# Issuing the work of two Mamba stages in a set order on each engine

## The chip, the cores and the metric

One NeuronCore of a Trainium2 chip runs the whole program. The metric is the device time of one execution in microseconds. The kernel before takes 16,464.6 us (median of four runs, 16,463.5 to 16,470.9). Executions of one kernel mostly agree here within 0.2%, and every run told below was of the fast state.

## The reference, cut to what matters

The program has three parts. Two of them are built on the Mamba recurrence: first two Mambas over one normalised input (4 images of 4096 steps), then one Mamba inside a block with two layer norms, a depthwise convolution and an MLP (4 images of 64 x 64). The third, a stage of windows, isn't touched.

```
def _mamba(x, ...):
    xc, z = split(x @ in_w.T)
    xc = silu(conv(xc) + conv_b)
    dt, B, C = split(xc @ x_w.T);  dt = softplus(dt @ dt_w.T + dt_b)
    # for every step t, 384 channels d, 16 states n:
    h = exp(dt[t] * A) * h + (dt[t] * xc[t]) * B[t]
    y[t] = sum over n of h * C[t]
    return ((y + D * xc) * silu(z)) @ out_w.T
```

Every step is float32. The recurrence can't be reordered along t; 384 x 16 rows of it are independent.

## The kernel before

A *unit* is 512 steps of one Mamba: 64 units in stage one (32 pairs, two Mambas for each piece of input), 32 in stage two. In a unit there are 12 *quads* of four scans. A quad goes through all the engines: a product on VectorE, four decays on ScalarE (Exp, into one of three buffers in PSUM, where this kernel also puts the results of its matmuls), four scans on VectorE, a multiplication with C on GpSimd (the *read* of h), and a sum over n on TensorE. One scan with its decay is a *tile*, 48 in a unit.

```
def scan(self, u, first, background):                 # one unit, cut
    for c in range(ND):
        for i, (o, q) in enumerate(...):              # a quad
            ... load dtE, dtxE ...
            nc.vector.tensor_tensor(h, dtxE, B, ALU.mult)              # product
            for j in range(4):
                nc.scalar.activation(dA, dtE[:, j, :], AF.Exp, scale=A)  # decay
                nc.vector.tensor_tensor_scan(h[:, j, :], dA, h[:, j, :], state, ...)
                background.step()                     # one piece of other work
            nc.vector.tensor_copy(self.state[:, n, :], h[:, :, T - 1])
            nc.gpsimd.tensor_tensor(h, h, C, ALU.mult)                 # read
            ... four matmuls: the sum ...
        nc.vector.scalar_tensor_tensor(y, xc, D, ys, ...)              # skip
    background.drain()
    nc.gpsimd.tensor_tensor(y, y, z, ALU.mult)                         # gate
```

All other work (norms, projections, convolution, Silu, Softplus, MLP) is a generator whose pieces are issued one after each scan. The *front* of a unit is what must be done before its scans, the *back* and *tail* are what comes after.

Of the kernel before, what the change touches and what calls it, by code (L numbers as in the profile page):

```python
# [119 lines left out]

class Norm:
# [98 lines left out]
class Mamba:  # L220
# [3 lines left out]
    def __init__(self, nc, name, taps, ins, const, work, psum, psum_y, psum_a, dram, ident, ex):  # L224
# [24 lines left out]

    def front(self, xn, first, u):  # L250

        nc, K = self.nc, self.taps
# [5 lines left out]
        for e in range(2 * ND):  # L258
            ps = self.psum.tile([128, T], F32, name="ps_in", tag="mm")
            for k in range(2):  # L260
                nc.tensor.matmul(  # L261
                    ps, self.in_w[:, k, bass.ts(e, 128)], xn[:, k, :], start=(k == 0), stop=(k == 1)
                )
            nc.scalar.copy(raw[:, e, K - 1 :] if e < ND else z[:, e - ND, :], ps)  # L264
            yield
        nc.gpsimd.tensor_copy(self.halo, raw[:, :, T:])
        xc = u["xc"] = self.work.tile([128, ND, T], F32, name="xc", bufs=2)
        for d in range(ND):
# [5 lines left out]
            nc.scalar.activation(xc[:, d, :], ps, AF.Identity, bias=self.conv_b[:, d : d + 1])  # L274
            yield
# [7 lines left out]
        nc.scalar.copy(dbl, ps)  # L283
# [3 lines left out]
        for d in range(ND):  # L287
            ps = self.psum.tile([128, T], F32, name="ps_dt", tag="mm")
            nc.tensor.matmul(ps, self.dt_w[:, bass.ts(d, 128)], dbl[:RK, :], start=True, stop=True)
            nc.scalar.activation(dt[:, d, :], ps, AF.Identity, bias=self.dt_b[:, d : d + 1])  # L290
        yield
        nc.scalar.activation(dt, dt, AF.Softplus)  # L292
        u["rows"] = []
        for i, v in enumerate((dt, dtx)):
            if i:
                nc.gpsimd.tensor_tensor(dtx, dt, xc, ALU.mult)  # L296
            r = self.dram.tile([DI, T], F32, name=("r_dt", "r_dtx")[i], bufs=3)
            u["rows"].append(r)
            rows = r.rearrange("(c q dd j) t -> q j dd c t", c=ND, q=2, j=4)
            for q in range(2):  # L300
                for j in range(4):
                    p = 32 * j + 16 * q
                    nc.sync.dma_start(rows[q, j], v[p : p + 16])
            yield

    def spread(self, u):

        nc = self.nc
        u["B"], u["C"] = [], []
        for o in range(2):  # L310
            B = self.psum_a.tile([128, T], F32, name=f"B{o}", bufs=1)
            nc.tensor.matmul(B, self.ex.spread[:, o, :], u["dbl"], start=True, stop=True)
            u["B"].append(B)
            ps = self.psum.tile([128, T], F32, name="ps_C", tag="mm")
            nc.tensor.matmul(ps, self.ex.spread[:, 2 + o, :], u["dbl"], start=True, stop=True)
            Cs = self.work.tile([128, T], F32, name=f"C{o}", bufs=2)
            nc.scalar.copy(Cs, ps)
            u["C"].append(Cs)

    def scan(self, u, first, background):  # L320
        nc = self.nc
        if first:
            nc.vector.memset(self.state, 0.0)
        self.spread(u)
        y = u["y"] = self.work.tile([128, ND, T], F32, name=f"{self.name}_y", bufs=1)
        xc, z = u["xc"], u["z"]
        at = 0
        for c in range(ND):
            ys = self.psum_y.tile([128, T], F32, name="y")
            octets = (0, 1) if c % 2 == 0 else (1, 0)  # L330
            for i, (o, q) in enumerate([(o, q) for o in octets for q in range(2)]):
                if i < 2:
                    wide = []
                    for r, n in zip(u["rows"], ("dtE", "dtxE")):
                        t = self.work.tile([128, 4, T], F32, name=n, bufs=2)
                        row = c * 128 + q * 64
                        nc.sync.dma_start(
                            t,
                            r[row : row + 64, :]
                            .rearrange("(dd j) t -> dd (j t)", j=4)  # L340
                            .unsqueeze(1)
                            .broadcast_to([16, 8, 4 * T]),
                        )
                        wide.append(t)
                    u[q] = wide
                dtE, dtxE = u[q]
                n = (c * 2 + o) * 2 + q
                h = self.work.tile([128, 4, T], F32, name="h", bufs=3)
                nc.vector.tensor_tensor(  # L349
                    h, dtxE, u["B"][o].unsqueeze(1).broadcast_to([128, 4, T]), ALU.mult  # L350
                )
                for j in range(4):
                    dA = self.psum_a.tile([128, T], F32, name="dA", bufs=3)
                    nc.scalar.activation(dA, dtE[:, j, :], AF.Exp, scale=self.A[:, n, j : j + 1])  # L354
                    nc.vector.tensor_tensor_scan(  # L355
                        h[:, j, :], dA, h[:, j, :], self.state[:, n, j : j + 1], ALU.mult, ALU.add
                    )
                    background.step()
                nc.vector.tensor_copy(self.state[:, n, :], h[:, :, T - 1])  # L359
                nc.gpsimd.tensor_tensor(  # L360
                    h, h, u["C"][o].unsqueeze(1).broadcast_to([128, 4, T]), ALU.mult
                )
                for j in range(4):
                    nc.tensor.matmul(  # L364
                        ys[32 * j : 32 * j + 32, :],
                        self.ex.gather[:, q, :],
                        h[:, j, :],
                        start=(i == 0),
                        stop=(i == 3),
                    )  # L370
            nc.vector.scalar_tensor_tensor(  # L371
                y[:, c, :], xc[:, c, :], self.D[:, c : c + 1], ys, ALU.mult, ALU.add
            )
        background.drain()
        nc.gpsimd.tensor_tensor(y, y, z, ALU.mult)  # L375


def two_mambas(tc, x, g, b, m_ins, ex_aps, out):
# [3 lines left out]
    with ExitStack() as ctx:  # L382
# [9 lines left out]
        eps = const.tile([128, 1], F32, name="eps")  # L392
        nc.vector.memset(eps, EPS)
# [3 lines left out]
        ex = Expand(nc, const, *ex_aps)  # L397
        mambas = [
            Mamba(nc, f"m{i}", 4, m_ins[i], const, work, psum, psum_y, psum_a, dram, ident, ex)
# [8 lines left out]
        def norm(u):  # L408
# [7 lines left out]
            nc.scalar.activation(rs, mv[:, :, 1], AF.Sqrt, bias=eps)  # L416
            nc.vector.reciprocal(rs, rs)
            yield
            xs = u["xs"] = work.tile([128, nq, C], F32, name="xs", bufs=2)
            for q in range(nq):  # L420
                nc.vector.tensor_scalar(
# [6 lines left out]
                )  # L428
            for i, op in ((0, ALU.mult), (1, ALU.add)):
# [5 lines left out]
            for k in range(2):  # L435
# [5 lines left out]
                nc.scalar.copy(xT[:, k, :], ps)  # L441
                yield

        def front(u, i):
            if i == 0:
                yield from norm(u)
            u[i] = {}
            yield from mambas[i].front(u["xT"], u["t"] == 0, u[i])

        def back(u):  # L450
            o = work.tile([128, nq, C], F32, name="o", bufs=2)
            for q in range(nq):
# [10 lines left out]
                nc.vector.tensor_tensor(o[:, q, :], ps, u["xs"][:, q, :], ALU.add)  # L463
                yield
            rows = out[u["b"], bass.ts(u["t"], T), :]
            nc.sync.dma_start(rows.rearrange("(q p) c -> p q c", p=128), o)
            yield

        background = Background()
        units = [{"b": bi, "t": t} for bi in range(NB) for t in range(NT)]  # L470
        load(units[0])
# [488 lines left out]
```

## Time and profile before

| part | us | a unit |
|---|---|---|
| stage one, first scan 98 to last skip 7676 | 7578 | 118 |
| stage two, 7798 to last scan 12,897 | 5099 | 159 |
| windows | 3395 | - |

In the views PE is TensorE, DVE VectorE, ACT ScalarE, POOL GpSimd, and SPq the queue of the sync engine, which issues the transfers; L355 is line 355 of the kernel. The two views below are VectorE's waits, in the kernel before: in each line stands the waiting instruction, whom it waited for, the sum in us, how often, and the longest. First stage one (500 to 7500 us):

```profile
DVE h L355 <- ACT dA L354: 789.4, 72, 25.5
DVE m_y L371 <- PE y L364: 381.6, 120, 7.2
DVE h L349 <- PE y L364: 129.4, 82, 5.9
```

then stage two (8000 to 12,500 us, some 27 units):

```profile
DVE ln_d L140 <- PE mean L138: 525.5, 40, 23.1
DVE img L559 <- PE ps_out L552: 416.2, 53, 45.9
DVE m_y L371 <- PE y L364: 278.3, 48, 21.1
```

In stage one a few long waits for the decay (72, up to 25 us) make up about half of VectorE's idle 1627 us. In stage two no wait is the main one: norm, output projection and skip each take 10 to 19 us of a unit. Keep these names for the comparison: after the change the names are others and the sum is much the same.

### The profile page before, as it was taken

The page shows a single profiled execution, that of the slowest core. Times are in us where ns is not written, and L with a number is a line of the kernel's source. Part 1 is how long each engine was busy: PE and PEld are TensorE (multiplying, and loading weights), DVE is VectorE, ACT ScalarE, POOL GpSimd, SP SyncE. Part 2 cuts the span into 40 slices and gives each one's busy share as a digit, 9 for nine tenths or more (in the row PEclk, how much of TensorE's full clock was granted, in tenths as well). Part 3 has the DMA queues.
Part 4 walks back from the last instruction along what each step waited for, and adds up shares of the span by engine and source line. Part 5 has one row for each costly group of instructions (what it writes and reads, how often), then busy time and mean ns, then how long its engine had stood idle before and what let it go on. Part 6 is the DMA issues. An engine that isn't in the chain of part 4 may idle for free.

```text
span 16446.6 us, 96745 instructions
## 1 busy us (share of the span) xinstructions
PE 11089.0 (67%) x34064; PEld 4801.7 (29%) x34064; DVE 9585.2 (58%) x9115; ACT 6342.4 (39%) x8392; POOL 6089.1 (37%) x1714
## 2 busy tenths in 40 slices
PE   5555556555555555565677777677777498998989
PEld 1112112111211211121222222222222165655656
DVE  6777877877787787786665656555656411112120
ACT  4444444444444444443444445444444211111111
POOL 4555555555555555554443434433434100000000
PEclk7666666666666666666677777777777699998989
DMA  5555555555555555554444444434434200000000
GB/s 129 118 120 118 128 120 119 127 120 119 119 126 120 117 125 122 120 130 105 106 94 89 93 88 94 101 82 92 97 88 90 53 10 6 10 6 10 6 2 6
DMA packets 366749, 1449.36 MB, mean 88 GB/s; under 512 B 95402, under 2 KB 128462, under 8 KB 218710
## 3 DMA queue, kind: packets, MB, share of 16 engines
q1 hardware_dynamic: 365502, 1440.02, 39.7%
q8 instruction: 268, 4.39, 0.1%
q10 hardware_dynamic: 760, 3.16, 0.1%
q14 instruction: 219, 1.79, 0.0%
HBM read 1254.25 MB, written 188.74 MB: 88 GB/s over the span
## 4 chain that ended last, share of the span: by engine, by line
PE 38%; DVE 28%; POOL 12%; DMA 8%; issue 7%; ACT 6%; SPq 0%; POOLq 0%; ACTq 0%; DVEq 0%
DVE h L355 18%; POOL h L360 10%; PE plus L726 6%; PE minus L726 5%; DVE h L349 5%; DMA dtE<-r_dt 4%; PE y L364 4%; DMA dtxE<-r_dtx 3%; PE ps_h L187 3%; PE ps_dw L576 3%; PE ps_conv L271 3%; PE ps_in L261 3%; PE ps_o L196 3%; POOL m_y L375 2%; ACT dA L354 2%
## 5 line engine op out<-in xcount | busy, mean ns | idle before, releaser
L360 POOL TENSOR_TENSOR h<-h,C 128x2048 f32<-128x2048 f32 x1152 | 5204.0, 4517 | 4399.1 <-DVE m_state L359 4207.4
L355 DVE TENSOR_TENSOR_SCAN h<-dA,m_state,h 128x512 f32<-128x512 f32 x4608 | 5556.8, 1263 | 1121.4 <-ACT dA L354 1115.1
L354 ACT ACTIVATE dA<-dtE,m_A 128x512 f32<-128x512 f32 x4608 | 3097.3, 687 | 3839.3 <-DVE h L355 2923.3
L364 PE MATMUL y<-h,gather 128*32 128x512 f32 x9216 | 1976.0, 900 | 3440.0 <-POOL h L360 3287.0
L349 DVE TENSOR_TENSOR h<-dtxE,B 128x2048 f32<-128x2048 f32 x1152 | 2612.2, 2273 | 622.4 <-PE y L364 277.7
L364 PEld LDWEIGHTS y<-h,gather 128*32 128x32 f32 x9216 | 226.9, 128 | 4812.9 <-POOL h L360 4369.9
L726 PE MATMUL plus<-xn,t 96*96 96x256 f32 x4352 | 1013.6, 380 | 0.0
L261 PE MATMUL ps_in<-xT,m_in_w 96*128 96x512 f32 x1536 | 848.1, 694 | 214.5 <-ACT z L264 197.5
L271 PE MATMUL ps_conv<-raw,m_conv 128*128 128x512 f32 x2112 | 980.6, 616 | 7.7 <-ACT z L264 6.6
L737 DVE TENSOR_TENSOR y<-plus,neg 96x512 f32<-96x512 f32 x64 | 44.0, 687 | 1597.1 <-ACT neg L736 1597.1
L726 PE MATMUL minus<-xn,t 96*96 96x256 f32 x3840 | 922.8, 392 | 10.8 <-ACT xn L169 10.7
L187 PE MATMUL ps_h<-xn,t 96*128 96x512 f32 x1536 | 802.1, 666 | 79.9 <-ACT xn L169 69.3
L726 PEld LDWEIGHTS plus<-xn,t 96*96 96x96 f32 x4352 | 710.1, 163 | 338.4 <-issue 133.1
L196 PE MATMUL ps_o<-hid,t 128*96 128x512 f32 x1536 | 739.3, 638 | 53.4 <-ACT hid L192 53.4
L726 PEld LDWEIGHTS minus<-xn,t 96*96 96x96 f32 x3840 | 638.2, 168 | 244.0 <-ACT xn L169 26.6
L664 POOL MEMSET img<- 96x132 f32 x4 | 0.8, 206 | 1788.2 <-DVE xw L711 1788.2
L371 DVE SCALAR_TENSOR_TENSOR m_y<-xc,m_pack,y 128x512 f32<-128x512 f32 x288 | 212.7, 738 | 738.8 <-PE y L364 738.8
L456 PE MATMUL ps_out<-m_pack,m_y 128*128 128x192 f32 x1536 | 413.7, 439 | 289.1 <-POOL m_y L375 184.0
L147 PE MATMUL var<-mean_w,xn 96*128 96x1 f32 x2048 | 357.4, 304 | 371.8 <-ACT xn L142 371.8
L271 PEld LDWEIGHTS ps_conv<-raw,m_conv 128*128 128x128 f32 x2112 | 416.0, 200 | 585.7 <-issue 547.4
L140 DVE TENSOR_TENSOR ln_d<-x,mean 96x1024 f32<-96x1024 f32 x96 | 116.5, 1214 | 744.3 <-PE mean L138 744.2
L296 POOL TENSOR_TENSOR dt_dtx<-dt_dtx,xc 128x1536 f32<-128x1536 f32 x96 | 329.2, 3429 | 551.7 <-ACT dt_dtx L292 551.7
(120 smaller groups left out, 11402.0 us busy)
## 6 DMA issues: line engine op xcount, KB each, us to landing
dtE<-r_dt SPq DMA_DIRECT2D x576, 1024.0 KB, 8.9
dtxE<-r_dtx SPq DMA_DIRECT2D x576, 1024.0 KB, 7.3
r_dt<-dt_dtx SPq DMA_DIRECT2D x768, 96.0 KB, 3.3
r_dtx<-dt_dtx SPq DMA_DIRECT2D x768, 96.0 KB, 3.0
x<-x SPq DMA_DIRECT2D x64, 384.0 KB, 3.9
xt<-in_x SPq DMA_DIRECT2D x32, 384.0 KB, 3.4
x<-o SPq DMA_DIRECT2D x32, 384.0 KB, 7.1
img<-x SPq DMA_DIRECT2D x8, 1536.0 KB, 21.2
```

What stands on the lines that cost most here:

```text
L187: nc.tensor.matmul(ps, self.w1[:, k, bass.ts(m, 128)], x[:, k, :], start=(k == 0), stop=(k == 1))
L196: nc.tensor.matmul(ps, self.w2[:, m, bass.ts(k, CP)], h[:, m, :], start=(m == 0), stop=(m == NH - 1),)
L261: nc.tensor.matmul(ps, self.in_w[:, k, bass.ts(e, 128)], xn[:, k, :], start=(k == 0), stop=(k == 1))
L271: nc.tensor.matmul(ps, self.conv[:, d, j, :], raw[:, d, j : j + T], start=(j == 0), stop=(j == K - 1))
L349: nc.vector.tensor_tensor(h, dtxE, u["B"][o].unsqueeze(1).broadcast_to([128, 4, T]), ALU.mult)
L354: nc.scalar.activation(dA, dtE[:, j, :], AF.Exp, scale=self.A[:, n, j : j + 1])
L355: nc.vector.tensor_tensor_scan(h[:, j, :], dA, h[:, j, :], self.state[:, n, j : j + 1], ALU.mult, ALU.add)
L360: nc.gpsimd.tensor_tensor(h, h, u["C"][o].unsqueeze(1).broadcast_to([128, 4, T]), ALU.mult)
L364: nc.tensor.matmul(ys[32 * j : 32 * j + 32, :], self.ex.gather[:, q, :], h[:, j, :], start=(i == 0), stop=(i == 3),)
L456: nc.tensor.matmul(ps, u[i]["y"][:, d, bass.ts(q, 128)], mambas[i].out_w[:, d, :], start=(i == 0 and d == 0), stop=(i == 1 and d == ND - 1),)
L576: nc.tensor.matmul(ps, dw[:, k, j, :], img[:, k, r + dy : r + dy + rows, dx : dx + HW], start=(j == 0), stop=(j == 8),)
L726: nc.tensor.matmul(ps[:, m, :], w["sed"][:, cc, s ^ k, bass.ts(m, CP)], xn[:, cc, bass.ts(s, NWIN)], start=(n == 0 and cc == 0), stop=(n = ...
```

## The change

Its intent: fix by hand in which order each engine gets its work, so that VectorE sees one stream of scans. The core of the diff, cut:

```diff
+class Scans:
+    AHEAD = 2
+        for i in range(n + 16):                       # every scan of the stage
+            self.step(i, n)
+            for fn in self.due.pop(i, []): fn()
+            r = i % (4 * NQ)
+            edge = (i + self.AHEAD) % 4 == 3
+            want = self.credit + self.behind.left / max(1, self.until(r) - r)
+            while want >= 1:                          # pieces of other work
+                if not self.behind.step(edge): break
+                want -= 1
+    def step(self, i, n):
+        ... load the pair two quads ahead ...
+        m2.decay(...)                                 # of tile i + AHEAD
+        m.step(u, k, j)                               # scan of tile i
+        if j == 3:
+            m.read(u, k)
+            m2.product(u2, k2)                        # of the next quad
+            self.at(i + 3, lambda: m.sum(u, k))
+            if k % 4 == 3:
+                self.at(i + 5, lambda: m.skip(u, c))
+                self.at(i + 7, lambda: m.gate(u, c))
+                if c == ND - 1: self.at(i + 7, after)
-                nc.vector.tensor_copy(self.state[:, n, :], h[:, :, T - 1])
+        nc.gpsimd.tensor_copy(self.state[:, k, :], h[:, :, T - 1])
...
-            nc.scalar.activation(rs, mv[:, :, 1], AF.Sqrt, bias=eps)
-            nc.vector.reciprocal(rs, rs)
+            nc.gpsimd.tensor_scalar(rs, mv[:, :, 1], EPS, None, ALU.add)
+            nc.gpsimd.tensor_tensor(rs, rs, minus_half, ALU.pow)
-                nc.vector.tensor_scalar(xs[:, q, :], xt[:, q, :], ...)
+                nc.gpsimd.tensor_scalar(xs[:, q, :], xt[:, q, :], ...)
...
+            Scans(nc, stream, behind, lambda r: 42).run()                  # stage one
+            Scans(nc, stream, behind, lambda r: 8 if r < 8 else 54).run()  # stage two
```

A piece may say `"burst"`: then the next piece (a Silu, Softplus or Gelu) waits for a quad edge. Before 253 of these 256 bursts the trace of the changed kernel shows a table load of 1.28 us, and before 250 decays another; the load at 3990.05 us is followed by its Silu at 3991.34. `later` puts the evacuation of a matmul's PSUM result one piece after the matmul. An *edge* is the tile at which the decay of a quad's last scan has just been issued, so that the next product (2.26 us of VectorE) gives ScalarE room. Not shown in the cut: both stages now run inside `tc.manual_schedule()`.

## The prediction

> **What bounds the kernel now.** I read the slices of the page first, to find the stages, then the groups, then the waits of each engine, then the timeline at the places that the change touches. The slices:
>
> ```profile
> DVE  6777877877787787786665656555656411112120
> ACT  4444444444444444443444445444444211111111
> POOL 4555555555555555554443434433434100000000
> PEclk7666666666666666666677777777777699998989
> DMA  5555555555555555554444444434434200000000
> ```
>
> One slice is 411 us. Three stages: two mambas (to slice 19), mamba block (to slice 32), windows. In the timeline the first scan starts at 98 us, the last skip of the two mambas is at 7676 us, the block's first continuous scans at 7798 us, its last scan ends at 12,897 us, and the window stage loads its first image at 13,052 us. So the 64 scan units of stage one take (7676 - 98)/64 = 118 us each, the 32 of stage two (12,897 - 7798)/32 = 159 us each, and 13,052 to 16,447 = 3395 us are window stage, which the diff leaves alone. No engine is full in the mamba stages: VectorE is the busiest in stage one, at 75% to 77%. The groups name its work:
>
> ```profile
> L355 DVE TENSOR_TENSOR_SCAN h<-dA,m_state,h 128x512 f32<-128x512 f32 x4608 | 5556.8, 1263 | 1121.4 <-ACT dA L354 1115.1
> L349 DVE TENSOR_TENSOR h<-dtxE,B 128x2048 f32<-128x2048 f32 x1152 | 2612.2, 2273 | 622.4 <-PE y L364 277.7
> L360 POOL TENSOR_TENSOR h<-h,C 128x2048 f32<-128x2048 f32 x1152 | 5204.0, 4517 | 4399.1 <-DVE m_state L359 4207.4
> L371 DVE SCALAR_TENSOR_TENSOR m_y<-xc,m_pack,y 128x512 f32<-128x512 f32 x288 | 212.7, 738 | 738.8 <-PE y L364 738.8
> ```
>
> The reader is to see that VectorE's scans and products are the longest work of the stages, and that its idle time is waits for others: 1115 us for ScalarE's decay, 739 us for the sum before each skip, 622 us ahead of products. GpSimd's 4.5 us per quad (a group of four scans) fits below VectorE's 7 us. What holds the decay back is shown at one place of the timeline:
>
> ```profile
> 3051.79 3.43 POOL L375 TENSOR_TENSOR m_y<-m_y,z 128x1536 f32<-128x1536 f32 x1 [2.09 <-DVE m_y L371]
> 3055.26 1.07 ACT L264 COPY z<-ps_in 128x512 f32<-128x512 f32 x2 [13.40 <-POOL m_y L375]
> 3078.91 1.28 DVE L355 TENSOR_TENSOR_SCAN h<-dA,m_state,h 128x512 f32<-128x512 f32 x1 [25.00 <-ACT dA L354]
> ```
>
> The copy of z waits 13.4 us in ScalarE's queue for the gate of the unit before, twelve decays and two table loads come after it, and VectorE stands for 25 us. These are waits by order, not by lack of an engine.
>
> [...] back to back, the product needs 2.21 us for 2048 columns and a scan 1.18 us for 512, so 1.08 against 2.3 ns a column. The scans are a floor that ordering can't lower. [...] at 7730.04 a load of 1.28 us is followed by its function at 7731.33. I count 1.28 us. [...] the eight matmuls of one sum take 1.06 us in dense stretches, 1.93 us after idling. [...] all 4608 scans lie between 1246 and 1285 ns, so moving work to GpSimd should not slow VectorE.
>
> **The change part by part.** *VectorE's floor.* The timeline shows five scans in 5.98 us, so (5.98 - 1.26)/4 = 1.18 us a scan, and 2.21 us from product start to scan start: a quad is 4 x 1.18 + 2.21 = 6.93 us, a unit 12 x 6.93 = 83.2 us, and three skips make 85.4. Stage one keeps statistics and residual adds, 1.5 us a unit: floor 87 us. State copies (175 us per 50 units, 3.5 us each) and the normalisation (94 us per 50, 1.9 us each) go to GpSimd, which stays near 70 us a unit. Stage two keeps two layer norms (4 x 1.21) and four adds (2.8 us): floor 93 us.
>
> *Decay two ahead.* With three buffers a decay may start when the scan three tiles before it has ended, and a scan plus two may pass before it is needed: lead 2 x 1.18 - 0.69 = 1.7 us. At an edge (decay for the quad's fourth tile just issued) the product adds 2.21 and one more scan time is left over: about 4.3 us. A Softplus burst is 1.28 + 1.48 + 1.28 = 4.0 us and fits. Silu is 1.28 + 2 x 1.48 + 1.28 = 5.5 us: 1.2 us over. In the next four tiles ScalarE has a decay and a copy per tile (0.69 + 0.6 = 1.3 us against 1.18), so it doesn't regain its lead and Softplus then also stalls: I count 1.2 + 0.8 + 1.4 = 3.4 us a unit.
>
> *Stage one.* Pieces are issued at left/(42 - r), 0.57 to 0.7 per scan, so a piece (four matmuls, 1.7 us warm, 3.4 cold) finds 1.8 us a scan of room on TensorE; late evacuations that hold ScalarE I take as 3.6 us a unit (my estimate, one late pair of copies per quarter of a unit). Loads: 2 MB a pair, landing in 7.3 to 8.9 us against 12 to 14 us of notice; the first pair of a unit waits for the row writes (issued from r = 35, nine microseconds of queue): 1 us. Sum 87 + 3.4 + 3.6 + 1 = 95 us, against 118: 64 x 23 = 1470 us gained.
>
> *Stage two has a trap.* The function `after(n)`, which adds the next output projection, front and tail, runs seven tiles after a unit's last, at r = 6 of the next unit. There the pace is left/(8 - r): 65 pieces left over 2, so 32 pieces fall due in one scan step and go on until the first burst mark. Counting the pieces through the loop: output projection (3), layer norm (8), input projection (6) and convolution (6) are all issued at r = 6, in order, on every engine. VectorE's scan 7 stands behind the norm's multiply, and decay 9 behind the copies of a convolution whose matmuls depend on the norm. The length of that chain is in the trace of before, where the block's second front runs without scans:
>
> ```profile
> 7753.61 3.73 PE L138 MATMUL mean<-x,mean_w 96*96 96x512 f32 x4
> 7757.43 1.22 DVE L140 TENSOR_TENSOR ln_d<-x,mean 96x1024 f32<-96x1024 f32 x1 [41.85 <-PE mean L138]
> 7768.23 12.61 PE L261 MATMUL ps_in<-xn,m_in_w 96*128 96x512 f32 x24 [2.21 <-ACT xn L169]
> 7788.60 0.69 ACT L274 ACTIVATE xc<-ps_conv,m_pack 128x512 f32<-128x512 f32 x1 [1.89 <-PE ps_conv L271]
> ```
>
> From 7753.6 to 7789.3 are 35.7 us; ahead stands the output projection (6.8 us in the drain at 12,909.9), behind it one decay (0.7). Of these 43 us VectorE uses 1.4 (adds) + 2.4 (norm) + two scans 2.4 + one product 2.2 = 8.4. Stall: 35 us a unit. After it the rest is even, 0.85 pieces a scan. There the tail costs: a depthwise piece is six matmuls at 0.43 = 2.6 us against 1.8 us a step, so its copies come late (5 us); the second norm's subtract stands on VectorE while Gelu, GpSimd's add and the mean run (5 us); the final adds wait for the second MLP product (3 us); Silu and the wide Gelu (1.28 + 2.76 + 1.28 = 5.3) overrun by 1 us together. Sum 93 + 35 + 14 = 142 us, against 159: 32 x 17 = 550 us gained.
>
> *Total.* Start 95, stage one 64 x 95 = 6080, passage 122 as now, stage two 32 x 142 = 4544, drain of the last two tails 155 as now, windows 3395: 14,391 us, 2070 us or 12.6% less than 16,465.
>
> **The rivals.** *The floor is reached.* If pieces fit everywhere and the heap at r = 6 is harmless, units take 90 and 100 us: 95 + 5760 + 122 + 3200 + 155 + 3395 = 12,727. For it: each engine but VectorE has 20% or more to spare. Against: [...] the chain above is made of real dependencies. *TensorE becomes the bound in stage two.* It is busy 74% of 159 us, 117 us a unit, at a granted clock of 0.74. If that stayed, nothing below 117 is possible, and with scans queued behind pieces 160 and 105 us a unit would give 95 + 6720 + 122 + 5120 + 155 + 3395 = 15,607. [...] *Transfers become the bound.* Stage one moves 121 GB/s at a share of 0.54; at 95 us a unit this is 0.54 x 118/95 = 0.67. That isn't full, but loads bunch at pair starts; late ones would add 3 us a unit, some 300 us.
>
> **Range and chances.** The two unit times carry it: 5 us in stage one are 320 us, 12 us in stage two are 384 us. Both low together give 13,690, both high 15,095; they aren't fully tied, so 13,650 to 15,000 holds it 8 times in 10. A gain under 2% needs almost all of both gains to vanish: faster 0.97, same 0.02, slower 0.01. Predicted: 14,390 us.
>
> **What would show it.** VectorE's share in stage one should be about 0.9, idle ahead of scans on the decay about 400 us in stage one. Waits of the skip on the sum should nearly vanish (739 to under 100 us). In stage two each unit should show one hole of 30 to 40 us in the scans, with norm, projection and convolution running in it; the norm's subtract should wait on its mean about 10 us at that place and 5 us in the tail. If stage two shows no hole and units near 105 us, my reading of the pace is wrong; if stage one is near 105 us with ScalarE waiting on TensorE, I undersized late pieces; if the first product of a unit waits on its rows, transfers.

## The result and the profile after

The changed kernel takes **15,174.7 us** (median of four, 15,172.5 to 15,177.0) against 16,464.6: ratio 0.9216, 95% interval 0.9200 to 0.9232. A ratio is the mean time of one kernel's fast runs over that of the other's of the same rounds, so not quite the ratio of the medians. It is 7.8% faster, in place of the predicted 12.6%, and 175 us above the top of the range.

Slices of the changed kernel, one slice now 379 us:

```profile
DVE  7888888888889888755556655555654303030210
...
POOL 5667666667666666544434434433443000000000
```

Stage one now ends in slice 17 of 40, VectorE is at 80% to 90% in it (before 75% to 77%), and GpSimd, which took over work, at some 69% (3794 of 5500 us). In stage two (slices 18 to 31) VectorE's digit is mostly 5 or 6, as it was before.

| | before | after |
|---|---|---|
| last residual add of stage one | 7688 | 6398 |
| from there to the last scan of stage two | 5208 | 5224 |
| from there to the end | 3550 | 3550 |

The whole gain of 1290 us is stage one's. Stage two, predicted to give 550 us, gave nothing. By the prediction's way of counting, stage one takes (6388.2 - 92.6)/64 = 98.4 us a unit (predicted 95). Stage two, from its first scan at 6487 to the end of its last at 11,623, takes 5136/32 = 160.5 (predicted 142; before 159.3).

VectorE's scans and products, to be held against the groups of before:

```profile
L525 DVE TENSOR_TENSOR_SCAN h<-dA,m_state,h 128x512 f32<-128x512 f32 x4608 | 5622.0, 1267 | 1489.5 <-ACT dA L519 1398.6
...
L510 DVE TENSOR_TENSOR h<-dtxE,B 128x2048 f32<-128x2048 f32 x1152 | 2603.6, 2260 | 308.0 <-DMA dtxE<-r_dtx 307.5
```

The durations are what they were (1267 against 1263 ns, 2260 against 2273): more work on GpSimd has not slowed VectorE. The idle time before scans has grown by 370 us, though, while that before products has halved. The group of the skips, whose wait for the sum was 738.8 us, has 17.1 us left. Where the waits went shows in stage two (7800 to 11,400 us; by the count of scans 21.8 units, of 165.4 us each, because the stage's first two units, of 119 and 133 us, lie outside):

```profile
DVE h L525 <- ACT dA L519: 544.7, 116, 19.3
DVE ln_d L198 <- PE mean L195: 352.1, 44, 15.2
DVE ln_d L228 <- PE rb L220: 205.3, 28, 8.3
DVE x L907 <- PE ps_o L266: 180.6, 28, 11.2
DVE h L510 <- DMA dtxE<-r_dtx: 123.6, 16, 8.7
DVE img L856 <- PE ps_out L848: 111.5, 44, 4.6
```

Divided by 21.8 units: 25.0 us of waiting for the decay, 16.2 and 9.4 for the two steps of a norm, 8.3 for the second MLP product (the final adds), 5.7 for a load, 5.1 for the output projection. Together 69.7 us a unit. VectorE is busy for 2046 us of the window, 94.0 a unit; its floor was predicted as 93. So the floor was right, and the waits were not: 70 in place of 49.

One unit of stage two in time; the columns are start, duration, engine, line, operation, tiles, and in brackets the idle time before and whom it ended with:

```profile
8724.23 0.31 SPq L827 DMA_DIRECT2D x<-x  x1
...
8728.31 3.70 PE L195 MATMUL mean<-x,mean_w 96*96 96x512 f32 x4 [4.84 <-DMA x<-x]
...
8732.05 1.22 DVE L198 TENSOR_TENSOR ln_d<-x,mean 96x1024 f32<-96x1024 f32 x1 [7.85 <-PE mean L195]
...
8741.55 1.22 DVE L228 TENSOR_TENSOR ln_d<-ln_d,rb 96x1024 f32<-96x1024 f32 x1 [8.29 <-PE rb L220]
...
8757.41 7.89 PE L433 MATMUL ps_conv<-raw,m_conv 128*128 128x512 f32 x18
...
8766.64 3.63 DVE L525 TENSOR_TENSOR_SCAN h<-dA,m_state,h 128x512 f32<-128x512 f32 x3 [19.18 <-ACT dA L519]
```

This is the predicted hole: at the seventh tile of the unit, output projection, norm, input projection and convolution stand one after another in front of a scan. With two waits for the output projection (3.17 and 1.89 us) VectorE idles 3.17 + 1.89 + 7.85 + 8.29 + 19.18 = 40.4 us. In 30 of the 32 units the waits from tile 5 to tile 10 add up to 39.6 to 41.4 us. What the prediction did not have is the first pair of lines: x of the unit after next is asked for only at 8724.23, inside the hole, and the mean waits 4.84 us for it. Later in the same unit:

```profile
8783.20 4.51 SPq L474 DMA_DIRECT2D r_dt<-dt_dtx  x8
8787.81 4.63 SPq L474 DMA_DIRECT2D r_dtx<-dt_dtx  x8
8792.49 0.52 SPq L494 DMA_DIRECT2D dtE<-r_dt  x1
...
8805.72 2.29 DVE L510 TENSOR_TENSOR h<-dtxE,B 128x2048 f32<-128x2048 f32 x1 [7.91 <-DMA dtxE<-r_dtx]
```

The sync engine issues the 16 writes of the rows of the next unit, 9.1 us of queue or 0.57 us each, and only then the load of the operands that the running unit needs; the product waits 7.91 us.

Stage one has one conspicuous place, once in a pair of units:

```profile
4138.32 3.98 POOL L697 TENSOR_SCALAR xs<-xt,mv,rs 128x192 f32<-128x192 f32 x4
...
4142.38 3.68 POOL L707 TENSOR_TENSOR xs<-xs,gb 128x768 f32<-128x768 f32 x2
...
4146.12 1.94 PE L715 MATMUL ps_t<-ident,xs 128*96 128x128 f32 x8 [7.24 <-POOL xs L707]
...
4147.24 0.58 ACT L718 COPY xT<-ps_t 96x512 f32<-96x512 f32 x1 [7.90 <-PE ps_t L715]
...
4149.30 2.46 DVE L525 TENSOR_TENSOR_SCAN h<-dA,m_state,h 128x512 f32<-128x512 f32 x2 [4.77 <-ACT dA L519]
```

GpSimd's normalisation (with the power in front, 1.04 us for 128 x 4 elements; 9 us in one block from 4136.9) holds the transposes back, these hold ScalarE's copy back, the copy holds the decays back, and VectorE stands for 4.77 us. The prediction had booked that move to GpSimd as free.

### The profile page after: what moved, and what is told of

It reads as the page before. It is cut to its first block, busy times and chain, and to the rows that moved or that the text cites. A ratio compares the mean times of both kernels' runs of the same rounds, so it can differ in the third digit from the quotient of the medians.

```text
span 15172.6 us, 97764 instructions
## 1 busy us (share of the span) xinstructions
PE 10805.9 (71%) x34064; PEld 4671.3 (31%) x34064; DVE 9262.7 (61%) x7740; ACT 6022.3 (40%) x8139; POOL 6543.0 (43%) x3314
## 4 chain that ended last, share of the span: by engine, by line
PE 37%; POOL 29%; issue 18%; DVE 8%; ACT 5%; DMA 3%; SPq 0%; POOLq 0%; DVEq 0%; ACTq 0%
POOL h L538 22%; PE plus L1050 6%; PE minus L1050 6%; PE ps_in L422 4%; DVE h L525 3%; PE ps_h L252 3%; PE ps_h L345 2%; PE ps_o L354 2%; PE ps_conv L433 2%; DMA dtxE<-r_dtx 2%; PE ps_o L266 2%; PE y L547 2%; POOL dt_dtx L465 2%; DVE h L510 2%; POOL m_y L564 1%
## 5 line engine op out<-in xcount | busy, mean ns | idle before, releaser
L525 DVE TENSOR_TENSOR_SCAN h<-dA,m_state,h 128x512 f32<-128x512 f32 x4608 | 5622.0, 1267 | 1489.5 <-ACT dA L519 1398.6
L538 POOL TENSOR_TENSOR h<-h,C 128x2048 f32<-128x2048 f32 x1152 | 5203.3, 4517 | 93.4 <-POOL m_state L537 1.6
L547 PE MATMUL y<-h,gather 128*32 128x512 f32 x9216 | 1704.0, 822 | 2100.4 <-POOL h L538 1975.9
L510 DVE TENSOR_TENSOR h<-dtxE,B 128x2048 f32<-128x2048 f32 x1152 | 2603.6, 2260 | 308.0 <-DMA dtxE<-r_dtx 307.5
L537 POOL COPY m_state<-h 128x4 f32<-128x4 f32 x1152 | 215.8, 187 | 2897.9 <-DVE h L525 2851.6
L422 PE MATMUL ps_in<-xT,m_in_w 96*128 96x512 f32 x1536 | 983.2, 798 | 0.0
L449 PE MATMUL ps_x<-xc,m_pack 128*44 128x512 f32 x576 | 454.4, 955 | 650.5 <-ACT xc L444 650.5
L422 PEld LDWEIGHTS ps_in<-xT,m_in_w 96*128 96x128 f32 x1536 | 372.7, 257 | 649.9 <-issue 466.1
L877 PE MATMUL ps_dw<-img,dw 96*96 96x512 f32 x1152 | 550.2, 631 | 14.1 <-ACT C L482 14.1
L195 PE MATMUL mean<-x,mean_w 96*96 96x512 f32 x256 | 236.7, 1079 | 384.0 <-POOL x L899 226.7
L1060 ACT COPY neg<-minus 96x512 f32<-96x512 f32 x64 | 36.7, 573 | 1166.7 <-PE minus L1050 1166.7
## 6 DMA issues: line engine op xcount, KB each, us to landing
dtxE<-r_dtx SPq DMA_DIRECT2D x576, 1024.0 KB, 11.3
```

The costliest lines, as they stand in the source:

```text
L422: nc.tensor.matmul(ps, self.in_w[:, k, bass.ts(e, 128)], xn[:, k, :], start=(k == 0), stop=(k == 1))
L449: nc.tensor.matmul(ps, self.x_w[:, d, :], xc[:, d, :], start=(d == 0), stop=(d == ND - 1))
L510: self.nc.vector.tensor_tensor(h, u[k // 2][1], u["B", k % 2].unsqueeze(1).broadcast_to([128, 4, T]), ALU.mult,)
L525: self.nc.vector.tensor_tensor_scan(h[:, j, :], u.pop(("dA", k, j)), h[:, j, :], self.state[:, k, j : j + 1], ALU.mult, ALU.add,)
L538: nc.gpsimd.tensor_tensor(h, h, u["C"][k % 2].unsqueeze(1).broadcast_to([128, 4, T]), ALU.mult)
L547: self.nc.tensor.matmul(u["ys"][32 * j : 32 * j + 32, :], self.ex.gather[:, i // 2, :], h[:, j, :], start=(i == 0), stop=(i == 3),)
```

## The experiments

All ran three rounds, all in the fast state, and all but the one marked are correct. "Stage one" is the start of its last residual add in the profiled run, "stage two" the time from there to its last scan (with some 90 us before its first scan, 110 in the kernel before).

| run | us | ratio to before | stage one | stage two |
|---|---|---|---|---|
| the change | 15,174.7 | 0.9216 | 6398 | 5224 |
| e1_even | 14,743.2 | 0.8958 | 6403 | 4787 |
| e3_ahead1 | 15,444.8 | 0.9385 | 6264 | 5624 |
| e4_old2 | 15,160.0 | 0.9212 | 6398 | 5200 |
| e5_prod | 15,587.9 | 0.9473 | 6613 | 5425 |
| e6_slack | 14,512.0 | 0.8813 | 6410 | 4545 |
| e7_slack_a1 | 14,383.4 | 0.8737 | 6279 | 4548 |
| e8_silu | 14,995.8 | 0.9108 | 6139 | 5302 |
| e9_prod_sum4 | 15,824.2 | 0.9612 | 6732 | 5539 |
| e10_best | 14,714.4 | 0.8936 | 6630 | 4530 |
| e11_prod_sum4b | 15,474.2 | 0.9401 | 6616 | 5305 |
| e12_tslack | 15,193.0 | 0.9227 | 6417 | 5226 |
| e13_rows | 15,202.0 | 0.9233 | 6395 | 5255 |
| e14_undo | 15,199.1 | 0.9229 | 6410 | 5235 |
| e15_noreload (wrong on purpose) | 14,937.1 | 0.9076 | 6397 | 5012 |
| e16_roworder | 15,094.6 | 0.9171 | 6395 | 5148 |
| e17_best | 14,087.2 | 0.8561 | 5997 | 4545 |
| e18_normat | 14,855.8 | 0.9027 | 6081 | 5223 |
| e19_normat_a1 | 14,912.9 | 0.9072 | 6142 | 5223 |

My theory after the result: the scheme is sound, and what it lost are dependent pieces issued too close behind each other, each of which costs its full latency because what was issued behind it on the same engine waits too (above, the copy that waited 7.90 us for the transposes held the decays behind it back, and a scan stood for 4.77). The rival: an engine is the bound in stage two (TensorE), and the waits only show that.

**Stage two: is it worth anything, and does the hole carry it?** e4_old2 keeps the old stage two in the new kernel (its scan method and generators, some 180 added lines, most of them a second class). e1_even changes one line:

```diff
-            Scans(nc, stream, behind, lambda r: 8 if r < 8 else 54).run()
+            Scans(nc, stream, behind, lambda r: 6 if r < 6 else 54).run()
```

> Stage one as in the changed kernel, stage two (mamba block) as it was before, with its own scheduler. By the scans in the two traces stage two takes 159 us a unit in both kernels, so the whole gain is stage one's: total 15,170 plus or minus 60 us. If the new stage two gains something that the scans don't show (its passage or its drain), this run is slower than the changed kernel by more than 100 us.

> Only the pace function of stage two is changed (leftovers due at tile 6, then all new pieces spread to tile 54), so the 24 pieces that fall due in one scan step are spread. Theory A (the heap at tile 6 makes the 40 us hole of each unit by order alone): the hole goes, some of it comes back as single waits of VectorE on the norm and of ScalarE on late copies; a unit falls from 159 to about 128 us, total about 14,200 us (13,900 to 14,500). Rival B (stage two is bound by TensorE's in-order work, 117 us busy a unit, and the hole is only where that shows): the waits move elsewhere, a unit stays above 150 us, total above 14,900 us.

e4_old2 took 15,160.0 us, as expected: rewriting stage two was worth nothing. e1_even took 14,743.2, so 431 us or 13.5 us a unit less: 147 us, between the forecasts of both theories. The hole is gone but for the units next to an image's edge, and the longest wait for a decay fell from 19.3 us to 9.8 (7200 to 10,400 us):

```profile
DVE h L525 <- ACT dA L519: 397.9, 164, 9.8
```

But only a third of the hole's 40 us came back. TensorE is not the bound, since the same matmuls now fit into less time, but my theory A was too simple: without the heap, the same dependences are spread over the unit and wait at other places.

**Slack between dependent pieces.** e6_slack adds to e1_even empty pieces where VectorE reads what TensorE was only just given, and issues the depthwise half of the tail ahead of the front:

```diff
             nc.tensor.matmul(mean, self.mean_w, x[:, k, :], ...)
-        yield
+        for _ in range(3):
+            yield
         nc.vector.tensor_tensor(d, x, mean..., ALU.subtract)
...                       # the same ahead of the multiplication by rb and of the final adds
+            behind.add(tail_a(b, t - 1, box), 7)          # depthwise, ahead of the front
             behind.add(front(u["next"]), ln.N + mamba.N)
-                behind.add(tail(b, t - 1), 8 + ln.N + mlp.N)
+                behind.add(tail_b(b, t - 1, box), 1 + ln.N + mlp.N)
```

> On top of the even pace of e1_even: in stage two the depthwise part of the tail is issued between the output projection and the next front (so that the reload of x and the add after Gelu lie far ahead of the norms), and three empty pieces stand between each TensorE result and the VectorE instruction that reads it in program order (mean and subtract, broadcast and multiply, second MLP product and final add). No instruction is added or taken away. Theory A (stage two is held by VectorE standing in order behind just issued work): of e1_even's waits a unit (subtract 11, multiply 7, final adds 12 us) some 22 us go; a unit falls from 146 to about 124 us, total about 14,050 us (13,850 to 14,350). Rival B (TensorE, busy 113 us of 146 a unit, is the bound now): the waits come back before other instructions, unit above 140 us, total above 14,550 us.

14,512.0 us, between the two. VectorE's waits over 3200 us of stage two (7200 to 10,400, 22.4 units):

```profile
DVE h L529 <- ACT dA L523: 596.2, 208, 13.5
DVE x L914 <- PE ps_o L268: 254.0, 44, 15.3
...
DVE ln_d L199 <- PE mean L195: 46.7, 22, 6.8
```

The wait for the mean fell to 46.7/22.4 = 2.1 us a unit, from 16.2 in the change and 251.3/21.0 = 11.9 in e1_even, and a unit takes 139 us in the mean of the stage. The waits for the decay went up from 397.9/21.0 = 18.9 us a unit in e1_even to 26.6. The run joins two edits, the empty pieces and the earlier depthwise half, and no run separates them. The predicted 142 is passed here, by another road than the change took.

**One tile ahead or two.** e3_ahead1 sets `AHEAD = 1`; e7_slack_a1 is e6_slack with `AHEAD = 1` in stage one only.

```diff
-    AHEAD = 2                                          # e3_ahead1
+    AHEAD = 1
...
-            Scans(nc, stream, behind, lambda r: 42).run()     # e7_slack_a1, on e6_slack
+            scans = Scans(nc, stream, behind, lambda r: 42)
+            scans.AHEAD = 1
+            scans.run()
```

> Decay one tile ahead in place of two, everything else as in the changed kernel. If the lead is what carries stage one's gain, each of ScalarE's 20 or so extra jobs a unit (0.6 to 1.5 us) delays a scan by about 0.3 to 0.7 us and each burst by 1.2 us more: stage one units grow from 98 to about 110 us, total about 15,900 us. If one stream and the even spread carry it and the lead is a detail: under 3 us a unit, total under 15,450 us.

> As e6_slack, with decay one tile ahead in stage one alone (two in stage two). In e3_ahead1 stage one ended 134 us earlier than in the changed kernel and stage two took 404 us longer. If the two stages are independent, this run is 134 us (100 to 160) faster than e6_slack. If one tile ahead only helped stage one by chance of the whole order, no difference beyond 40 us.

e3_ahead1 was 270 us slower, in two opposite parts that neither forecast had: stage one ended 134 us earlier, stage two took 400 us longer. e7_slack_a1 kept the gain of stage one: 14,383.4, 129 us less than e6_slack, as expected. So "decay two ahead" is not what made stage one faster. It seemed even to cost something; e19_normat_a1 below shows that this was wrong too.

**The product's place.** A scan that follows directly on its own product starts 2.36 us after the product's start; where a scan of the quad before follows, it starts after 2.18. The run asks whether the time between dependent instructions makes the difference. In the changed kernel:

```profile
4012.65 2.26 DVE L510 TENSOR_TENSOR h<-dtxE,B 128x2048 f32<-128x2048 f32 x1
4015.01 2.46 DVE L525 TENSOR_TENSOR_SCAN h<-dA,m_state,h 128x512 f32<-128x512 f32 x2
```

in e5_prod, which issues the product one scan earlier:

```profile
4006.12 2.27 DVE L510 TENSOR_TENSOR h<-dtxE,B 128x2048 f32<-128x2048 f32 x1
4008.30 4.80 DVE L525 TENSOR_TENSOR_SCAN h<-dA,m_state,h 128x512 f32<-128x512 f32 x4
```

```diff
+        if j == 2 and i + 2 < n:
+            m2, u2, k2, _ = self.tile(i + 2)
+            m2.product(u2, k2)
         if j == 3:
             m.read(u, k)
-            if i + 1 < n: ... m2.product(u2, k2)
```

> The product of the next quad is issued one scan earlier (after the third scan of the quad before), so that it no longer stands directly ahead of its own first scan. In the changed kernel product start to scan start takes 2.37 us, where product and scan belong to one quad, in place of 2.21 us in the kernel before, where they mostly don't. [...] 0.16 us x 1152 quads = 184 us less, about 14,990 us. If the 0.16 us comes from elsewhere (GpSimd's copy running at the same time): no change, 15,150 to 15,200 us.

The step is 2.18 us in place of 2.36, as expected, and yet the kernel was 413 us slower, at 15,587.9. In 5500 us of stage one the waits for the decay rose from 543 to 702 us and those of the residual adds from 17 to 86. Two more runs tried to mend this by issuing sum, skip and gate later:

```diff
-            self.at(i + 3, lambda: m.sum(u, k))
+            self.at(i + 4, lambda: m.sum(u, k))
-                self.at(i + 5, lambda: m.skip(u, c))
+                self.at(i + 6, lambda: m.skip(u, c))
-                self.at(i + 7, lambda: m.gate(u, c))      # e9_prod_sum4 only; also `after`
+                self.at(i + 8, lambda: m.gate(u, c))
```

> e5_prod (product one scan early) with sum, skip and gate one tile later. In e5_prod the next quad's scans follow at once, so three scans after a quad are 3.5 us, less than GpSimd's read of 4.7 us, and TensorE stands in its order at the sum while ScalarE waits for pieces behind it. If this made e5_prod slower (stage one ended at 6,613 us against 6,398): with the sum four scans later it ends at about 6,280 us, the 0.16 us a quad now being gained, and the total is 15,000 to 15,200 us. If the early product itself breaks the bursts: stage one still ends after 6,550 us.

> As e5_prod, with the sum four and the skip six tiles behind, the gate and all that follows left at seven. In e9_prod_sum4 the waits of ScalarE for TensorE's pieces did fall (copies of C, raw and z behind the sum: from 757 to under 60 us in 5,500), but the gate, moved to eight, made the copies of z wait (236 us) and the residual adds too (193 us). If the early sum was what made e5_prod slow, stage one now ends near 6,300 us and the total is about 15,050 us (14,950 to 15,250). If the early product itself is at fault, stage one ends after 6,500 us again and the total is above 15,450 us.

Neither mended it: 15,824.2 and 15,474.2, with stage one at 6732 and 6616. Both met their second forecast, that the early product itself is at fault. In e9_prod_sum4 the copies of z waited for the later gate, and the residual adds for 193 us. Why an early product costs so much stays open. I can only argue that everything behind GpSimd then has 2.2 us less distance to its producer.

**Shorter bursts.** e8_silu splits the Silu burst into two, one for xc and one for z, each (1.28 + 1.48 + 1.28 = 4.0 us) shorter than the lead of the decays at an edge, 4.3 us by the prediction's estimate:

```diff
         nc.scalar.activation(xc, xc, AF.Silu)
-        nc.scalar.activation(z, z, AF.Silu)
         yield
...
             rows.append(r)
-            yield
+            yield "burst" if i else None
+        silu_z()                                   # the Silu of z taken out above
+        yield
```

> The changed kernel with the Silu burst split in two: xc's Silu at its edge, z's at a later edge after the row writes. Each burst is then 1.28 + 1.48 + 1.28 = 4.0 us, within the 4.3 us of an edge; a unit has one table load more. If the overrun of the wide burst and the lost lead after it make the waits before scans (about 5.6 us a unit in stage one: 1.23, 1.22, 1.73, 1.38), 3 to 5 us a unit go there: stage one ends near 6,150 us in place of 6,398, total 14,850 to 15,000 us. If ScalarE's waits on TensorE's results make them, they stay: total within 60 us of 15,175, or slower by the loads.

Stage one ended at 6139, 259 us earlier, as expected; waits for the decay in the 5500 us fell from 543 to 312 us. In stage two it cost some 80 us. More than the burst changed, though: one piece more shifts the later pieces of the unit.

**Adding up what helped, first try.** e10_best takes e7_slack_a1, the split Silu in stage one, and empty pieces ahead of the transposes and the final adds:

```diff
-            for _ in range(3):                         # on e7_slack_a1: ahead of the final adds
+            for _ in range(3 if k else 9):
...                                                    # normalisation to transposes
-            yield
+            for _ in range(5):
+                yield
...                                                    # split Silu as in e8_silu, stage one only
+        if self.name != "m":
+            nc.scalar.activation(z, z, AF.Silu)
```

> The parts that helped, together: even pace and empty pieces in stage two (as e6_slack, with six more ahead of the first final add), one tile ahead and a split Silu burst in stage one, four empty pieces between GpSimd's normalisation and the transposes. If the gains of the two stages add up: from 14,383 (e7_slack_a1) the split Silu takes about 200 and the empty pieces of stage one about 100, the later final adds about 150: 13,950 us (13,800 to 14,150). If the extra empty pieces crowd the real ones and the waits come back elsewhere: 14,250 or more.

14,714.4 us, worse than e7_slack_a1: stage one ended at 6630. The gains did not add. I take it that each edit that changes counts moves where all the later pieces fall; the run doesn't show which of its parts did the harm. From here on I preferred edits that leave the counts alone.

**The missed terms.** e12_tslack and e13_rows still were of the old kind: four empty pieces ahead of the transposes, three ahead of the row writes.

```diff
                     xs, xs, gb[:, i, :]..., op)            # e12_tslack
-            yield
+            for _ in range(5):
+                yield
...
+        for _ in range(3 if self.name == "m" else 0):      # e13_rows
+            yield
         rows = []
```

> The changed kernel with four empty pieces between GpSimd's normalisation (9 us of GpSimd work that the change moved there) and the transposes that need it. In the changed kernel ScalarE stands up to 7.9 us at the copy of the transpose in every other unit and a scan waits 4.8 us for its decay. If order alone makes this: 4 to 5 us a pair of units go, 32 pairs: total about 15,030 us (14,990 to 15,080). If GpSimd's time is the limit there: 15,150 or more.

> The changed kernel with three empty pieces ahead of the row writes in stage two alone, so that the load of the fourth pair (issued at tile 16) stands ahead of the 16 writes in the transfer queue and not behind them. If the 7.5 us wait of each unit's seventh product on its load (5.5 us on average) is this queue's order: about 5 us a unit, total 15,010 us (14,960 to 15,070). If the load is late by bandwidth, or the wait passes to the next pair: within 40 us of 15,175.

Neither gained (15,193.0 and 15,202.0). In e13_rows the wait for the load vanished from 3200 us of stage two (7800 to 11,000; 107 us to none) and the wait for the decay rose by 177. In e12_tslack GpSimd's block then stood ahead of a read, the sum waited 13 us for that read, and the transposes stood behind the sum in TensorE's order. Four runs took the same terms without touching the counts of stage two:

```diff
# e15_noreload (wrong result on purpose)
-                behind.later(lambda: load(u["next"]))
+                u["next"]["x"] = u["x"]
# e16_roworder: in stage two, the two copies of C are issued ahead of the row writes
+        if self.name == "m":
+            ... C ...
+            ... rows ...
# e14_undo
-                nc.gpsimd.tensor_scalar(xs[:, q, :], ...)
+                nc.vector.tensor_scalar(xs[:, q, :], ...)
# e18_normat: the seven pieces of the normalisation leave the common queue
+                        pieces = norm(after)
+                        for r in (9, 13, 15, 19, 23, 27, 31):
+                            scans.at(scans.now + r, lambda: next(pieces))
```

> Wrong result on purpose: in stage two the next unit's x is never loaded, the tile of the first unit serves for all, no instruction else is added, removed or moved. Theory (the reload of x stands in the chain of the hole): the mean of the norm no longer waits 4.8 us for the load, the hole falls from about 40 to about 35 us, 32 x 4.8 = 154 us less: 15,020 us, within 40. Rival (the load lies beside another wait of the same chain, which then takes its place): the time stays within 30 us of 15,175.

14,937.1 us, 238 less, more than the expected 154. The mean no longer waits for a load, and the subtract that waited 7.85 us has this line left:

```profile
8782.07 1.22 DVE L198 TENSOR_TENSOR ln_d<-x,mean 96x1024 f32<-96x1024 f32 x1 [1.03 <-PE mean L195]
```

With 4.53 + 1.89 + 1.03 + 8.29 + 17.78 us the hole is 33.5 us, against a prediction of 35; over the units it is 30.6 to 33.6 us, the first and last left out. Apart from the reload, the chain was read rightly. The 6.9 us that this hole lost would be 32 x 6.9 = 221 of the 238 us.

> In stage two the two copies of C are issued ahead of the row writes, the number of pieces unchanged, so that the operands of the fourth pair are asked for ahead of the 16 writes in the SP queue. Theory (queue order makes the load late): the wait of 5.5 us a unit for the load vanishes and nothing else moves, 32 x 5 = 160 us less: about 15,015. Rival (the stall only moves: ScalarE without a lead stalls at the next copies as in e13_rows, or the first pair of the next unit waits for its rows): within 40 us of 15,175.

15,094.6 us, 80 less, half of what was expected. The wait for the load is gone (5.7 us a unit to none), but 3.6 us came back: waits for the decay and the mean are up by 2.3 and 1.3 us a unit (7800 to 11,400 us, 21.8 units in the change and 22.3 here). Both theories hold by halves.

> In stage one the seven pieces of GpSimd's normalisation are placed one to a quad, straight behind a read, in place of wherever the counts of pieces put them. Theory (a block of 9 us of GpSimd's work delays the read of h, the sum on TensorE and the transposes behind it, 2.4 us a unit): 64 x 2.4 = 150 us less, about 15,025, and the wait of scans at the transposes of 4.8 us a pair falls below 2. Rival (the transposes wait for something else, or the read is late by the one piece as well): within 40 us of 15,175.

14,855.8 us, 319 less, all of it in stage one and twice what was expected. Waits over the same 5500 us of stage one, the change:

```profile
DVE h L525 <- ACT dA L519: 543.2, 348, 4.8
```

and e18_normat:

```profile
DVE h L525 <- ACT dA L519: 291.9, 208, 2.0
```

The long waits are gone (longest 2.0 in place of 4.8 us), and the short ones at bursts have become fewer. A unit takes 93.4 us, better than the 95 of the prediction. Taking seven pieces out of the queue also moved others, so the 319 us are the block and that shift together; the run does not divide them.

> One word changed: the four scalings of a pair's normalisation in stage one run on VectorE again in place of GpSimd (4 us of the block of 9). The prediction's own sum would have it slower by 64 x 1 to 64 x 1.3 us, 15,240 to 15,260. If the block on GpSimd costs more than the work on VectorE: the wait at the transposes falls from 4.8 to about 1 us a pair, VectorE takes 2 us a pair (four short instructions) more: 32 x 2 = 60 us faster, 15,110.

15,199.1 us: neither theory. The wait at the transposes did go, but VectorE now waits for the power on GpSimd, 112.6 us in the 5500 (4 us a pair):

```profile
DVE h L525 <- ACT dA L519: 400.1, 279, 1.9
DVE xs L697 <- POOL rs L694: 112.6, 28, 4.0
```

Where the scaling runs hardly matters, as long as the power stays on GpSimd in front of it; where in the order the block falls matters more (e18_normat).

e19_normat_a1 asks the question of one tile or two again, with the block in its place:

```diff
             scans = Scans(nc, stream, behind, lambda r: 42)    # on e18_normat
+            scans.AHEAD = 1
             scans.run()
```

> e18_normat with the decay one tile ahead in stage one. If one ahead is better in itself (less stands between two decays on ScalarE), another 60 to 130 us off e18_normat's 14,856: 14,730 to 14,800. If its gain in e3_ahead1 was only a shift of pieces against the block of normalisation: within 40 us of 14,856, or slower.

14,912.9 us (14,907.7 to 14,989.1), 57 slower than e18_normat. So one tile ahead is not better in itself: its gain in e3_ahead1 hung on the block in the common queue, and with the block in its place two ahead is better by 60 us in stage one. That it was a shift of the pieces against the block fits both runs, but isn't shown by itself.

**Adding up, second try.** e17_best has e6_slack's stage two, the split Silu in stage one and the placed normalisation; but for the counts of pieces no line in it is new:

```diff
-            Scans(nc, stream, behind, lambda r: 8 if r < 8 else 54).run()
+            Scans(nc, stream, behind, lambda r: 6 if r < 6 else 54).run()
+            ... the empty pieces and tail_a, tail_b of e6_slack ...
+            ... pieces = norm(after), placed at 9, 13, 15, ... as in e18_normat ...
+        if self.name != "m": nc.scalar.activation(z, z, AF.Silu)   # its own burst
```

> What helped, together: the even pace in stage two with three empty pieces ahead of dependent VectorE work, Silu split into two bursts in stage one alone, normalisation pieces one to a quad. If gains add: e6_slack 14,512 less 259 for the split Silu and 150 for the normalisation, 14,100 us. If piece counts shift the rest again as in e10_best: above 14,383, the best so far.

14,087.2 us (14,078.5 to 14,099.7), ratio 0.8561, 95% interval 0.8548 to 0.8573: the best version, 14.4% faster than the kernel before and 7.2% faster than the change. The total is as expected, its parts aren't: stage one gained 401 us in place of 409, but the placed block is 317 of it (150 expected) and the split Silu only 84 once the block is placed. Alone it had shown 259. That the two errors cancel is luck.

## Why the prediction was wrong

The direction and the mechanism were right; the size was 784 us off, 218 in stage one (64 x 3.4), 592 in stage two (32 x 18.5), less 23 in the passage between them (99 us for 122), because the second front now runs among the first scans.

*VectorE's floor* was right: 87 and 93 us predicted, 98.4 less its waits of (543.2 + 17.5)/55.7 units = 10.1, so 88.3, and 94.0 busy measured. The 1.3 us in stage one can all be the pause between a product and its own scan: the prediction had taken product to scan as 2.21 us from the old order, the lines at e5_prod have 2.36, and 12 x 0.15 = 1.8 us (an estimate).

*Decay two ahead* was half right. The burst waits are 1.23, 0.72, 1.73 and 1.38 us in one unit (1.42 for 0.72 in the next), so some 5.4 us: near the 1.2 + 0.8 + 1.4 = 3.4 predicted but for one term of 1.7, before which ScalarE waits for TensorE's results. The lead at an edge that this rests on, "about 4.3 us", doesn't come out of its own terms (1.7 + 2.21 + 1.18 = 5.1). And being two ahead was not what carried the gain: one ahead ended stage one earlier in e3_ahead1, and only 60 us later than e18_normat in e19_normat_a1.

*Stage one*, "Sum 87 + 3.4 + 3.6 + 1 = 95 us": loads cost 0.0 in place of 1; all waits for the decay are 9.7 in place of 3.4 + 3.6 = 7.0. The bursts are some 5.4 of them, a late copy of C 1.2 (4018.68 us; 3.6 had been estimated for late copies), and the wait behind GpSimd's block 4.77 us a pair of units, so 2.4. The step that failed is "the normalisation ... go to GpSimd, which stays near 70 us a unit". The share came out as said (3794/55.7 = 68 us), but a share of busy time was read as permission: the block of 9 us at one place costs, whatever the share (e18_normat: 93.4 us a unit, with the shift of the other pieces in it).

*Stage two*, "Sum 93 + 35 + 14 = 142 us", is where the prediction failed. The step that failed is the sum of waits, 35 + 14 = 49 us: the runs show 70. The trap itself was read rightly from the loop, and so was its chain: 33.5 us without the reload. The terms that were too small, in us a unit:

| term | predicted | measured |
|---|---|---|
| hole | 35 | 40.4 |
| decay outside the hole (depthwise, Silu, Gelu) | 5 + 1 | 25.0 - 19.2 = 5.8 |
| norms outside the hole | 5 | (16.2 - 7.85) + (9.4 - 8.3) = 9.5 |
| final adds | 3 | 8.3 |
| load behind the row writes | 0 | 5.7 |
| sum | 49 | 69.7 |

(The hole's 19.2, 7.85 and 8.3 are those of the unit shown; the rest are means.) The hole's excess is the reload of x: without it the hole is 33.5 us (e15_noreload). I had taken x as loaded, because two units were loaded at the start. The load of a quad's operands stands behind 16 writes in its queue, which I had counted for stage one ("nine microseconds of queue") and forgotten for stage two; but taking its wait away gave only 2.5 us a unit of the 5.7 (e16_roworder). Norms and final adds I had sized each by itself, 5 and 3 us. The even pace, empty pieces and the earlier depthwise half together took the mean's wait from 16.2 to 2.1 us a unit (e6_slack); that the short distance between producer and reader in the order is what cost fits this, but the run doesn't divide its edits. The final adds did not come down in that run (254.0/22.4 = 11.3 us), so what holds them up stays open. And the predicted gain was a small difference of large waits: before, VectorE's seven largest waits in stage two, three of which are shown above, add up to 1761/27.3 = 64.5 us a unit, after they are 69.7. Of VectorE's own work the change took only 96.5 - 94.0 = 2.5 us a unit. One wait took the place of another.

*The rivals.* The floor (12,727) was never near. TensorE as the bound would have made 15,607, and the 160 us of stage two look like it, but e6_slack does the same matmuls in 139. Transfers as a bound: in stage one their waits are 0.9 us in 5500.

*What would show it.* VectorE's share in stage one is 4880/5500 = 0.89 (predicted about 0.9). The skip's wait for the sum is 17 us in all (under 100). One hole a unit of 40 us (30 to 40). The subtract waits 7.85 and 5.89 us (about 10 and 5). Idle before scans in stage one is some 620 us, 9.7 x 64 (about 400). Four of the five signs of the mechanism were right or nearly, and the sum was not: signs of a mechanism don't bound the terms beside it.

*One reading* was off without harm. At the copy of z (3055.26 us) no decays follow: eight other instructions of ScalarE and two table loads stand before the next decay at 3078.19.

The two speeds of TensorE that the prediction counts with are in the trace of before. Of 145 sums from 2000 to 3500 us, 40 took 1.06 or 1.07 us, with a median of 0.0 us of TensorE's idle time just before them, and 102 took 1.93 or 1.94, with a median of 3.9. The four matmuls of a mean took 1.96 us at 8416.84, straight behind other matmuls, and 3.73 at 8045.41, after 4.49 us of idle time. Four matmuls at the 0.43 us of a depthwise piece (15.47 us for 36) make the 1.7 us of the prediction's piece; its 3.4 lies near the 3.36 of a mean at 13,001.18. What sets the speed isn't shown.

## What to carry to other kernels

When work is issued in a fixed order by counts, look for the places where the count empties its queue at once (here left/(8 - r)), and for every piece ask not how busy its engine is but what stands between it and its producer on each engine it passes. A long block on an engine that has time to spare can cost too, if something in order waits behind it (4.77 us a pair of units here). To size a term, edit one dependence with all counts left alone: edits that change counts move other pieces as well, and their gains and losses need not add (e10_best).
